# Cross attention on one core: transposing the probabilities by transfers of 16-bit halves instead of on TensorE

## The chip, the core and the metric

The kernel runs on one core of a Trainium2 chip. The metric is the device time of one execution, in microseconds. The core has TensorE (PE, with its weight load shown apart as PEld), VectorE (DVE), ScalarE (ACT), GpSimd (POOL) and SyncE (SP), whose queue issues nearly all transfers of this kernel. Each engine works through its instructions in order; semaphores tie the engines together.

## The reference

The program is one layer of three parts on a latent array x of 16 batches x 64 latents x 512: cross attention to a context of 16 x 512 x 512, a differential self attention over the 64 latents, and a feed-forward with blockwise 4-bit quantisation of activations and weights. Only the first part is touched. With 8 heads of 64, per batch:

```python
xn = _ln(x, g_x, b_x)            # context, 512 rows
ln = _ln(latents, g_l, b_l)      # 64 rows
q = ln @ w_q
kv_in = jnp.concatenate([xn, ln], axis=1)
k, v = jnp.split(kv_in @ w_kv, 2, axis=-1)
sim = jnp.einsum('bhid,bhjd->bhij', q * scale, k)
sim = jnp.where(m, sim, -jnp.finfo(sim.dtype).max)
attn = jax.nn.softmax(sim, axis=-1)
out = jnp.einsum('bhij,bhjd->bhid', attn, v)
return _ln(out @ w_out, g_o, b_o)
```

So each head has 64 queries against 512 context keys and 64 latent keys. The last product contracts over the keys, and TensorE contracts over partitions; the probabilities are computed with the queries on the partitions and must be transposed first. All is float32.

## The kernel before, in words

A first stage (latents) makes the latents' queries, keys and values and parks them in DRAM. Then cross_attention (line 860) loops over the 16 batches, and self attention and feed-forward follow. The order of instructions on each engine is that of the program text; everything below stands where the author of the loop wrote it.

In batch b, PE works through these products. keys(b, m), four times (line 932, tile pk): 12 matmuls of 128x128x512, three terms of a high and low split of float32 over four chunks; DVE evicts the result, times the row of reciprocal deviations (L941). scores(b, a), for a = 0 and 1 (line 957, tile sim): 16 small matmuls each, four heads at a time in two PSUM tiles r = 0, 1, where the partitions are two heads x 64 queries. softmax (line 975): DVE adds the mask and takes the extreme (L986), ACT makes the exponentials and their sum (L990), into the tile pr of 128 x 2 x 576 float32, with the 512 context keys and 64 latent keys of each r in one row. values(b, t), four times (line 944, tile pv): 12 matmuls of 128x128x512, evicted by ACT with a scale (L954).

The products with the values follow one batch later: in batch b, finish(b - 1) (line 1135) does weigh_latents and four times weigh (L1055, tile av), which read the transposed probabilities. These are made in turn(b - 1) (line 994), between keys(b, 0) and keys(b, 1): 32 PE transposes of 64x128 blocks (L1004, tile prt) into the PSUM tiles that the scores use, and four ACT copies (L1013) to the tiles prT in SBUF. turn_latents (line 1016) behind it does the same for the latent keys with two transposes (L1023, tile prlt) and one copy (L1024). In odd batches from 3 on, out_turn (tile ot, copies oh at L1090), and later out_product (tile po) finish a pair of batches.

Beside this run, in the same loop: the next context's split into high and low parts (cx.high on ACT, L362; cx.low on DVE or POOL, L368), the statistics of the context after that on DVE (L321), and the weights' quantiser (Quantise.tick, which advances jobs by one step at each call): a load on SP, then DVE and POOL steps, an ACT step (L205), more DVE, a transposition on DVE (L287), an ACT cast (L288), a subtraction on DVE (L290) and a store on SP (L293).

SP's queue also holds, per batch: four fetches of the raw context (L354), the load of the context in its other layout (nat, L314), the latents' keys (eight small ones, L929 and L930), the row (L347), and in begin(b + 1) the mask bytes mu (L897) and the queries (L899), then the latents' values (L909). ACT turns mu into the mask at the end of the batch (L913).

Pools: pr has two buffers, prT four, the PSUM tiles of pk, pv and po share three, the scores' pair has two.

Of the kernel before, what the change touches and what calls it, by code (L numbers as in the profile page):

```python
# [9 lines left out]
F32 = mybir.dt.float32  # L10
F32R = mybir.dt.float32r
U32 = mybir.dt.uint32
U8 = mybir.dt.uint8
AF = mybir.ActivationFunctionType
ALU = mybir.AluOpType
AX = mybir.AxisListType
# [3 lines left out]
P = 128  # L20
D = 512
KC = D // P
B = 16
S = 64
N = 512
NJ = N // P
# [24 lines left out]
class Common:  # L51
# [808 lines left out]
def cross_attention(tc, cm, sc, i, cw, cx, w1, w2, att, quant):  # L860

    nc = tc.nc
# [24 lines left out]
    state = {}  # L887
    half = (N + S) // 2

    def begin(b):  # L890
        if b >= B:
            return
        p, e = divmod(b, 2)
        g, n = divmod(b, GB)
        mine = slice(n * S, (n + 1) * S)
        mu = w1.tile([P, N], U8, tag="mu", name=f"mu_{b}")
        nc.sync.dma_start(mu, i["mask"][b : b + 1, :].to_broadcast([P, N]))  # L897
        with nc.allow_non_contiguous_dma(reason="the latents of a batch"):
            nc.sync.dma_start(queries[e], sc.q[g][:, :, mine])  # L899
        state[b] = dict(mu=mu, k=[], v=[], tot=cm.small.tile([P, KC], F32, tag="tot", name=f"tot_{b}"))  # L900

    def latents_values(b):
        if b >= B:
            return
        p, e = divmod(b, 2)
        vl = state[b]["vl"] = w2.tile([P, KC, S], F32, tag="two_l", bufs=2, name=f"vl_{b}")
        src = sc.v[p][e * S : (e + 1) * S].rearrange("p (n two d) -> p n two d", two=2, d=S)
        for h in range(2):
            nc.sync.dma_start(vl[h * S : (h + 1) * S], src[:, :, h, :])  # L909
# [22 lines left out]
    def keys(b, m):  # L932

        k = ends.pop((b, m))
        hi, lo = cx.done[b]
        cols = slice(m * P, (m + 1) * P)
        ps = cm.mm(f"pk_{b}_{m}")
        cm.product(
            ps, lambda c: (w_k[0][:, c, cols], w_k[1][:, c, cols], hi[:, c, :], lo[:, c, :]), range(KC)
        )  # L940
        nc.vector.tensor_tensor(k[:, S : S + N], ps, cx.row[b], ALU.mult)  # L941
        state[b]["k"].append(k)

    def values(b, t):
        hi, lo = cx.done[b]
        cols = slice(t * P, (t + 1) * P)
        ps = cm.mm(f"pv_{b}_{t}")
        cm.product(
            ps,
            lambda k: (hi[:, k, cols], lo[:, k, cols], w_v[0][:, k, :], w_v[1][:, k, :]),  # L950
            range(KC),
        )
        v = w1.tile([P, D], F32, tag="v", bufs=4, name=f"v_{b}_{t}")
        nc.scalar.mul(v, ps, cx.rs[b][:, t : t + 1])  # L954
        state[b]["v"].append(v)
# [18 lines left out]

    def softmax(b, a):
        st = state[b]
        st["pr", a] = w1.tile([P, 2, N + S], F32, tag="pr", bufs=2, name=f"pr_{b}_{a}")

        def two(t):
            return t.rearrange("p (h n) -> p h n", h=2)  # L980

        for r, ps in enumerate(st.pop(("sim", a))):
            mask = masks[b % 2][:, columns_of(r)[0]]
            pr = st["pr", a][:, r, :]
            least = cm.small.tile([P, 1], F32, tag="least", name=f"least_{b}_{a}_{r}")
            nc.vector.tensor_tensor_reduce(  # L986
                two(pr), ps[:, :, :half], two(mask), -1.0, BIG, ALU.add, ALU.min, least
            )
            t = 2 * a + r
            nc.scalar.activation(  # L990
                pr, pr, AF.Exp, bias=least, scale=-1.0, accum_out=st["tot"][:, t : t + 1]
            )

    def turn(b):

        pts = [cm.two(f"prt_{b}_{a}") for a in range(2)]
        for a, pt in enumerate(pts):
            for r in range(2):
                first = columns_of(r)[1].start
                for j in range(NJ):  # L1000
                    at = (r * NJ + j) * S
                    for c in range(2):
                        rows = slice(c * S, (c + 1) * S)
                        nc.tensor.transpose(  # L1004
                            pt[:, c, at : at + S],
                            state[b]["pr", a][rows, r, first + j * P : first + (j + 1) * P],
                            cm.ident[rows, rows],
                        )
        for a, pt in enumerate(pts):
            for r in range(2):  # L1010
                prT = w1.tile([P, NJ, P], F32, tag="prT", bufs=4, name=f"prT_{b}_{a}_{r}")
                src = pt[:, :, r * NJ * S : (r + 1) * NJ * S].rearrange("p c (j q) -> p c j q", q=S)
                nc.scalar.copy(prT.rearrange("p j (c q) -> p c j q", q=S), src)  # L1013
                state[b]["prT", a, r] = prT

    def turn_latents(b):
        st = state[b]
        prl = w2.tile([P, 2, P], F32, tag="two_h", bufs=2, name=f"prl_{b}")
        pt = cm.ps_av.tile([P, D], F32, tag="av", name=f"prlt_{b}")[:, : 2 * P]
        pt = pt.rearrange("p (n q) -> p n q", q=P)  # L1020
        for a in range(2):
            pr = st.pop(("pr", a)).rearrange("p r t -> p (r t)")
            nc.tensor.transpose(pt[:, a, :], pr[:, N : N + P], cm.ident)  # L1023
        nc.scalar.copy(prl, pt)  # L1024
        st["prl"] = prl

    def weigh_latents(b):

# [92 lines left out]
    def out_moments(p):  # L1121
        cm.shift(cm.x[p], f"a_{p}", cm.x_mv[:, p, :])
# [29 lines left out]
    for b in range(B):  # L1152

        def tick():
            if b:
                quant.tick()

        done = (b - 3) // 2 if b >= 3 and b % 2 else None
        last = b == B - 1
        keys(b, 0)  # L1160
        if last:
            att.load("Wq")
            att.load("Wk")
        cx.high(b + 1, 0)
        if b >= 4 and b % 2 == 0:
            out_moments((b - 4) // 2)
        if b > 1:
            tick()
        if b:
            turn(b - 1)  # L1170
            turn_latents(b - 1)
        if done is not None:
            out_turn(done)
        keys(b, 1)
        cx.low(b + 1, 0)
        cx.high(b + 1, 1)
        if b > 1:
            tick()
        keys(b, 2)
        if done is not None:  # L1180
            out_low(done)
        cx.fetch(b + 2, 0)
        if b == 0:
            for k in range(KC):
                load_o(k)
        cx.flat(b + 1)
        cx.low(b + 1, 1)
        cx.high(b + 1, 2)
        tick()
        if last:  # L1190
            att.split("Wq", 0, 1)
        if b == 0:
            scores(b, 0)
            softmax(b, 0)
        keys(b, 3)
        cx.fetch(b + 2, 1)
        if b:
            scores(b, 0)
            softmax(b, 0)
        cx.low(b + 1, 2)  # L1200
        cx.high(b + 1, 3)
        if b:
            finish(b - 1)
            scores(b, 1)
            softmax(b, 1)
            around(b + 1, 2, 3)
            around(b + 2, 0, 1)
        tick()
        values(b, 0)
        cx.every(b + 1)  # L1210
        cx.low(b + 1, 3)
        cx.stats(b + 2, 0)
        tick()
        if last:
            att.split("Wq", 2, 3)
            att.load("Wv")
        if b == 0:
            scores(b, 1)
            softmax(b, 1)
            around(b + 1, 2, 3)  # L1220
            around(b + 2, 0, 1)
        values(b, 1)
        begin(b + 1)
        latents_values(b + 1)
        cx.fetch(b + 2, 2)
        cx.stats(b + 2, 1)
        tick()
        if last:
            att.norm(0)
            att.split("Wk", 0, 1)  # L1230
        tick()
        if done is not None:
            out_product(done)
        tick()
        values(b, 2)
        cx.fetch(b + 2, 3)
        cx.stats(b + 2, 2)
        tick()
        if done is not None:
            out_norm(done)  # L1240
            out_add(done)
        if b == 0:
            weight_o(0)
            weight_o(1)
        if b == 2:
            att.sa.load()
        if b == 5:
            att.sa.work()
        if last:
            att.split("Wk", 2, 3)  # L1250
            att.load("Wo")
            att.turn(0)
        values(b, 3)
        cx.stats(b + 2, 3)
        cx.spread(b + 2)
        mask(b + 1)
        if b == 0:
            weight_o(2)
            weight_o(3)
        quant.tick()  # L1260
        cx.load(b + 3)
# [693 lines left out]
```

## Time and profile before

| What | Value |
|---|---|
| Median of 3 runs | 879.98 us (879.5 to 880.17) |
| The profiled execution | 881.33 us |
| Its span, first to last instruction | 879.5 us |
| PE, PEld busy | 871.7 us (99%), 719.2 us (82%) |
| DVE, ACT, POOL busy | 687.2 us (78%), 398.8 us (45%), 296.2 us (34%) |
| PE prt L1004, 512 transposes | 226 ns each, pipelined; 2% of the chain that ended last |
| PE pv and pk L121 | 20% and 19% of that chain |
| ACT copies prT L1013, 64 | 594 ns each |
| SP's queue (q1) | 80136 packets, 109.48 MB, 38.2% of 16 engines |

The engines' times are those of one profiled execution; busy time of PE is that of pipelined matmuls, so what one of many in a row costs is read from the length of the row, not from the mean of one. The chain that ended last is followed back from the last instruction: what stands on it sets the end. The table of groups gives, for a line and an engine, the number, the busy time, the mean of one, and the idle time of the engine just before with what ended it. The first transposes stand at 110 us, the last at 553 us of the span.

### The profile page before, as it was taken

What the parts mean: (1) busy time and instruction counts of PE and PEld (TensorE: products, weight loads), DVE (VectorE), ACT (ScalarE), POOL (GpSimd) and SP (SyncE); (2) the same over time, 40 slices, a digit from 0 to 9 for tenths busy, and PEclk for the clock granted to TensorE, in tenths of its full rate; (3) what the DMA queues carried; (4) which work ended last, traced back from release to release, by engine and by line L of the source; (5) the groups of instructions that cost most, each with busy time, mean ns of one, the idle gap of its engine ahead of it and who ended that gap; (6) DMA issues with size and microseconds to landing.
All of it is one profiled execution on the core that took longest, in us unless ns stands there. A gap on an engine that the chain in (4) does not pass through costs nothing.

```text
span 879.5 us, 17521 instructions
## 1 busy us (share of the span) xinstructions
PE 871.7 (99%) x6743; PEld 719.2 (82%) x6743; DVE 687.2 (78%) x1457; ACT 398.8 (45%) x787; POOL 296.2 (34%) x341
## 2 busy tenths in 40 slices
PE   8999999999999999999999999999999999999998
PEld 8988787878787888778878888888888888888887
DVE  7734457789788887787888867688998897888876
ACT  5654454544544535354445455554556233332221
POOL 2334234235353352353433622545543120111100
PEclk9999999999999999999999999999999999999999
DMA  8464554644655455435644362240008330000000
GB/s 277 167 233 169 167 163 142 201 143 141 192 164 160 138 174 168 136 111 178 183 134 149 121 198 64 82 192 1 1 3 320 136 144 13 13 13 13 13 12 25
DMA packets 80379, 111.12 MB, mean 126 GB/s; under 512 B 33176, under 2 KB 39080, under 8 KB 79016
## 3 DMA queue, kind: packets, MB, share of 16 engines
q1 hardware_dynamic: 80136, 109.48, 38.2%
q8 instruction: 53, 0.87, 0.4%
q0 software_dynamic: 160, 0.52, 0.2%
q14 instruction: 30, 0.25, 0.1%
HBM read 84.26 MB, written 25.72 MB: 125 GB/s over the span
## 4 chain that ended last, share of the span: by engine, by line
PE 93%; DVE 3%; DMA 2%; ACT 1%; POOL 1%; issue 1%; SPq 0%; ACTq 0%; DVEq 0%; POOLq 0%
PE pv L121 20%; PE pk L121 19%; PE gu L121 13%; PE dn L121 6%; PE sim L967 4%; PE av L1055 4%; PE Wv L121 3%; PE wo L121 3%; PE po L121 2%; PE Wq L121 2%; PE Wk L121 2%; PE prt L1004 2%; PE lq L121 2%; PE lk L121 2%; PE lv L121 1%; PE ht L171 1%
## 5 line engine op out<-in xcount | busy, mean ns | idle before, releaser
L121 PE MATMUL pv<-xvh,x 128*128 128x512 f32 x512 | 133.0, 394 | 0.0
L121 PE MATMUL pk<-x,xkh 128*128 128x512 f32 x512 | 128.2, 392 | 0.0
L121 PEld LDWEIGHTS pv<-xvh,x 128*128 128x128 f32 x512 | 94.8, 188 | 26.2 <-issue 7.0
L121 PEld LDWEIGHTS pk<-x,xkh 128*128 128x128 f32 x512 | 94.9, 188 | 19.5 <-issue 0.4
L990 ACT ACTIVATE pr<-pr,least 128x576 f32<-128x576 f32 x64 | 49.1, 769 | 59.7 <-DVE least L986 59.7
L941 DVE TENSOR_TENSOR k<-pk,row 128x512 f32<-128x512 f32 x64 | 43.2, 675 | 39.2 <-PE pk L121 39.0
L368 POOL TENSOR_TENSOR x<-raw,x 128x512 fp32r<-128x512 f32 x32 | 41.6, 1301 | 85.8 <-ACT x L362 80.5
L121 PE MATMUL pv<-xvl,x 128*128 128x512 f32 x256 | 68.7, 390 | 0.0
L121 PE MATMUL pk<-x,xkl 128*128 128x512 f32 x256 | 68.5, 389 | 0.0
L954 ACT ACTIVATE v<-pv,rs 128x512 f32<-128x512 f32 x64 | 43.2, 684 | 54.8 <-PE pv L121 54.3
L121 PE MATMUL gu<-uT,fx 128*128 128x512 f32 (+1 forms) x288 | 67.0, 377 | 0.2 <-DMA uT<-u_d 0.2
L121 PE MATMUL gu<-gT,fx 128*128 128x512 f32 (+1 forms) x288 | 65.8, 376 | 0.0
L121 PEld LDWEIGHTS gu<-gT,fx 128*128 128x128 f32 x288 | 52.2, 188 | 7.6 <-ACT fx L129 0.2
L121 PEld LDWEIGHTS gu<-uT,fx 128*128 128x128 f32 x288 | 51.8, 188 | 7.7 <-DMA uT<-u_d 0.5
L121 PEld LDWEIGHTS pv<-xvl,x 128*128 128x128 f32 x256 | 48.0, 188 | 10.3
L121 PEld LDWEIGHTS pk<-x,xkl 128*128 128x128 f32 x256 | 48.1, 188 | 10.2
L986 DVE CUSTOM_DVE_ANT_0 pr<-sim,mask 128x576 f32<-128x576 f32 x64 | 45.8, 753 | 5.3 <-PE sim L967 4.3
L205 ACT ACTIVATE qe_h<-qe_h,mmagic 128x512 f32<-128x512 f32 (+1 forms) x24 | 16.5, 687 | 66.7 <-DVE qe_h L202 64.6
L321 DVE BATCH_NORM_STATS2 cst<-nat 128x6 f32<-128x512 f32 x64 | 42.8, 669 | 3.7 <-DMA nat<-in_ctx_dram 3.7
L121 PE MATMUL dn<-dT,hh 128*128 128x512 f32 x170 | 42.9, 392 | 0.0
L967 PE MATMUL sim<-k,mask 64*64 64x288 f32 x512 | 40.4, 415 | 0.3 <-DMA mask<-q_d 0.3
L362 ACT CAST x<-raw 128x512 fp32r<-128x512 f32 x64 | 39.1, 631 | 0.0
(347 smaller groups left out, 1867.1 us busy)
## 6 DMA issues: line engine op xcount, KB each, us to landing
nat<-in_ctx_dram SPq DMA_DIRECT2D x16, 1024.0 KB
raw<-in_ctxT_dram SPq DMA_DIRECT2D x64, 256.0 KB
d_d<-qhl_d SPq DMA_DIRECT2D x11, 512.0 KB
row<-rs_d SPq DMA_DIRECT2D x16, 256.0 KB
g_d<-qhl_g SPq DMA_DIRECT2D x8, 512.0 KB
u_d<-qhl_u SPq DMA_DIRECT2D x8, 512.0 KB
gT<-g_d SPq DMA_DIRECT2D x4, 1024.0 KB
uT<-u_d SPq DMA_DIRECT2D x4, 1024.0 KB
```

The costliest lines, as they stand in the source:

```text
L121: self.nc.tensor.matmul(ps, lhsT=p[i], rhs=p[j], start=start and n == 0, stop=stop and n == last)
L205: nc.scalar.activation(e, e, AF.Relu, bias=self.mmagic, scale=MAGIC)
L321: nc.vector.bn_stats(st, self.nat[b][:, j, :])
L362: self.cm.nc.scalar.copy(self.done[b][0][:, c, :], self.raw[:, c, :])
L368: by.tensor_tensor(lo, self.raw[:, c, :], f32(hi), ALU.subtract)
L941: nc.vector.tensor_tensor(k[:, S : S + N], ps, cx.row[b], ALU.mult)
L954: nc.scalar.mul(v, ps, cx.rs[b][:, t : t + 1])
L967: nc.tensor.matmul(pss[r][c * S : (c + 1) * S, h, :half], lhsT=queries[b % 2][rows, m, :], rhs=st["k"][m][rows, at : at + half], start=Tru ...
L986: nc.vector.tensor_tensor_reduce(two(pr), ps[:, :, :half], two(mask), -1.0, BIG, ALU.add, ALU.min, least)
L990: nc.scalar.activation(pr, pr, AF.Exp, bias=least, scale=-1.0, accum_out=st["tot"][:, t : t + 1])
L1004: nc.tensor.transpose(pt[:, c, at : at + S], state[b]["pr", a][rows, r, first + j * P : first + (j + 1) * P], cm.ident[rows, rows],)
L1055: nc.tensor.matmul(st["av"][r][rows, a, :], lhsT=prT[:, j, rows], rhs=st["v"][j][:, at : at + S], start=False, stop=j == NJ - 1, skip_grou ...
```

## The change

For batches 0 to 14, turn is no longer called. Instead, ACT splits the float32 probabilities of pr into two tiles of their low and high 16 bits (halves: two copies of 128 x 1024 words per a). SP issues a transposing transfer for each of the two (send), from 128 x 1024 words to eight transposed blocks of 128 x 128 in a tile far, which takes its place in pr's pool, and so its buffer. In the next batch ACT copies the transposed words back into their places in prT (join: four copies of 128 x 512 words per a), which weigh reads as before. A block's partitions are again the keys, its columns two heads x 64 queries. The last batch still uses turn.

pr and far are now one width (2 x 640 words), so that the context keys of both r can be seen as one regular pattern. turn_latents moves one batch earlier, behind values(b, 1), since pr's buffer is to be freed for far; its result is kept in the second half of the tile that holds the latents' values.

```diff
@@ latents_values(b)
-        vl = state[b]["vl"] = w2.tile([P, KC, S], F32, tag="two_l", bufs=2, name=f"vl_{b}")
+        both = w2.tile([P, 2, KC * S], F32, tag="two_l", bufs=2, name=f"lat_{b}")
+        vl = state[b]["vl"] = both[:, 0].rearrange("p (n d) -> p n d", d=S)
+        state[b]["prl"] = both[:, 1].rearrange("p (n q) -> p n q", q=P)
@@ softmax(b, a)
-        st["pr", a] = w1.tile([P, 2, N + S], F32, tag="pr", bufs=2, name=f"pr_{b}_{a}")
+        wide = w1.tile([P, 2 * (N + 2 * S)], F32, tag="pr", bufs=2, name=f"pr_{b}_{a}")
+        st["wide", a] = wide.rearrange("p (r n) -> p r n", r=2)
+        st["pr", a] = wide[:, : 2 * (N + S)].rearrange("p (r n) -> p r n", r=2)
@@ new functions
+    def halves(b, a):
+
+        st = state[b]
+        src = st.pop(("wide", a))[:, :, :N].bitcast(U16).rearrange("p r (n h) -> p h r n", h=2)
+        for h in range(2):
+            half = w2.tile([P, 2, N], U16, tag="two_h", bufs=2, name=f"half_{b}_{a}_{h}")
+            nc.scalar.copy(half, src[:, h])
+            st["half", a, h] = half
+
+    def send(b, a):
+
+        st = state[b]
+        far = w1.tile([P, 2 * (N + 2 * S)], F32, tag="pr", bufs=2, name=f"far_{b}_{a}")
+        far = far[:, : 2 * N].bitcast(U16).rearrange("p (h n q) -> p h n q", h=2, q=P)
+        for h in range(2):
+            half = st.pop(("half", a, h)).rearrange("p r n -> p (r n)")
+            nc.sync.dma_start(far[:, h], half, transpose=True)
+        st["far", a] = far
+
+    def join(b, a):
+
+        far = state[b].pop(("far", a))
+        for r in range(2):
+            prT = w1.tile([P, NJ, P], F32, tag="prT", bufs=4, name=f"prT_{b}_{a}_{r}")
+            dst = prT.bitcast(U16).rearrange("p j (q h) -> p h j q", h=2)
+            for h in range(2):
+                nc.scalar.copy(dst[:, h], far[:, h, r * NJ : (r + 1) * NJ])
+            state[b]["prT", a, r] = prT
@@ the loop over b, behind keys(b, 0)
         if b:
-            turn(b - 1)
-            turn_latents(b - 1)
+            join(b - 1, 0)
         if done is not None:
             out_turn(done)
         keys(b, 1)
+        if b:
+            join(b - 1, 1)
@@ behind values(b, 0)
+        if b and not last:
+            halves(b, 0)
@@ behind values(b, 1)
+        if b == 0:
+            halves(b, 0)
+        if not last:
+            turn_latents(b)
+            send(b, 0)
         begin(b + 1)
@@ behind values(b, 2)
+        if not last:
+            halves(b, 1)
+            send(b, 1)
```

More of the change, by code (lines that the diff above doesn't have):

```diff
@@ L13 @@
 U8 = mybir.dt.uint8
+U16 = mybir.dt.uint16
 AF = mybir.ActivationFunctionType
@@ L1014, in turn @@
                 state[b]["prT", a, r] = prT
+    def halves(b, a):
[21 more added lines that the diff above has]
+            state[b]["prT", a, r] = prT
     def turn_latents(b):
         st = state[b]
-        prl = w2.tile([P, 2, P], F32, tag="two_h", bufs=2, name=f"prl_{b}")
+        prl = st["prl"]
         pt = cm.ps_av.tile([P, D], F32, tag="av", name=f"prlt_{b}")[:, : 2 * P]
@@ L1024, in turn_latents @@
         nc.scalar.copy(prl, pt)
-        st["prl"] = prl
     def weigh_latents(b):
```

## The prediction

> **What bounds the kernel now.** I read the page first, then the chain of work that ended last in order of time, then the stretch that holds the cross-attention loop.
>
> ```profile
> PE 871.7 (99%) x6743; PEld 719.2 (82%) x6743; DVE 687.2 (78%) x1457; ACT 398.8 (45%) x787; POOL 296.2 (34%) x341
> ```
>
> TensorE (PE) is busy 99% of the span. The chain confirms that this is no average over idle stages: in the loop it never leaves PE. One even batch (6) of it:
>
> ```profile
> 254.91 2.72 PE pk L121 x12
> 257.63 1.14 PE prt L1004 x32
> 259.14 8.21 PE pk L121 x36
> 268.71 2.02 PE av L1055 x64
> 271.86 11.15 PE pv L121 x48
> 283.00 2.72 PE pk L121 x12
> ```
>
> The columns are start, length, what. The batch takes 283.00 - 254.91 = 28.09 us; the odd batch after it, with the output product, 314.57 - 283.00 = 31.57 us; the mean is 29.8. The 32 probability transposes (prt) stand on this chain with 1.14 us; the 0.37 us behind them are the latents' two transposes (prlt), which the change keeps. Before another engine is charged, its room must be known:
>
> ```profile
> 111.00:553.00 442.00, 442.00 (x3732) 355.09 (x3730) 350.37 (x785) 216.76 (x437) 177.01 (x195) 1.00 0.50 154
> ```
>
> This is the stretch of the loop: its length, then busy us (and instructions) of PE, its weight load, DVE, ACT, POOL, the clock, the DMA share, GB/s. PE 442 of 442; ACT 216.76, 49%; DVE 79%; the DMA engines half. The clock is 1.00 throughout, so no clock effect enters.
>
> **Removed.** Fifteen of the sixteen calls of turn (batch 15 keeps its own): 15 x 1.14 = **17.1 us** of PE, all on the path. On ACT, four copies out of PSUM per batch, 2.04 us as a train. The scores' PSUM pair is no longer borrowed; no view shows PE waiting for it, so that is worth nothing.
>
> **Added on ACT.** Nothing in this trace copies 16-bit words with a stride, so I take the rows with the same number of elements:
>
> ```profile
> L1013 ACT COPY prT<-prt 128x512 f32<-128x512 f32 x64 | 32.6, 594 | 0.0
> L362 ACT CAST x<-raw 128x512 fp32r<-128x512 f32 x64 | 39.1, 631 | 0.0
> L1456 ACT ACTIVATE ex<-ex 128x1024 f32<-128x1024 f32 x8 | 8.5, 1062 | 22.6 <-DVE ex L1447 22.6
> ```
>
> Behind one another they overlap: four copies of 594 ns run in 2.04 us, two casts in 1.18 us. halves: 4 x (1.062 - 0.084) = 3.9 us a batch. join: 8 x 0.59 = 4.7 us. Net 3.9 + 4.7 - 2.04 = +6.6 us a batch; ACT goes to 216.8 + 15 x 6.6 = 316 us of some 425, 74%. Bounds: half that time if narrow words run faster, twice if stride or width hurts. Twice would give 216.8 + 15 x (17.2 - 2.0) = 445 us, more than the stretch, and ACT would be the bound. I take the rows as they are, because the mask's activation, which reads one-byte words (715 ns, with bias and scale), costs about what the f32 ones of its size do (684 ns).
>
> Where these copies stand decides more than their sum. Let K be the start of a batch's first pk. In the new order ACT has behind the last pv: v, mask, one x cast, join 0 (2.4), in odd batches four oh (1.2), join 1 (2.4). That ends at K+8. PE needs the last joined tile after four pk (10.9), the first scores (1.1) and the latents' product: K+12.5. Cover: some 4.5 us. In batch 7 of the trace ACT reached its copies only at K+8, since in its order it stood behind a quantiser cast that waited for DVE:
>
> ```profile
> 290.51 0.62 ACT L288 CAST qhl_u<-qhl_u 128x512 fp32r<-128x512 f32 x1 [3.47 <-DVE qhl_u L287]
> 291.04 2.04 ACT L1013 COPY prT<-prt 128x512 f32<-128x512 f32 x4
> ```
>
> So even there join ends near K+13.5, just where weigh takes it. The halves stand behind v of pv 0 and of pv 2, 1.95 us each; the v behind them comes at most 0.3 us later than its pv, and three PSUM buffers cover that. turn_latents now stands behind pv 1 and makes PE wait for the second exp: that ends at about K+19.5, PE arrives at K+21.5. Batch 0 has its second scores only one pv (2.7 us) earlier: up to **+1 us**, once.
>
> **Added transfers.** Four transposes of 128 x 1024 words (256 KB) per batch. The trace holds none. From its packet records, by size: 256-byte packets take 17.9 ns each, 2048-byte ones 101 ns, 4-byte ones 9 ns. A block's row is 128 words, 256 bytes: 1024 packets x 17.9 / 16 engines = **1.15 us**. Low end: like long rows, 128 x 101 / 16 = 0.8 us. High end: each word its own packet, 131072 x 9 / 16 = 74 us. I take 1.15, the packet size that the tile's blocks have. Four make 4.6 us a batch; the DMA share goes from 0.50 to some 0.68.
>
> [...]
>
> On SP's queue, in order, the first pair waits for ACT's halves and for prlt, at K+21.5. It stands where the queue is now, behind the row:
>
> ```profile
> 304.69 0.58 SPq L347 DMA_DIRECT2D row<-rs_d  x1
> 305.31 0.42 SPq L897 DMA_DIRECT2D mu<-in_mask_dram  x1
> ...
> 308.38 0.43 SPq L281 DMA_DIRECT2D qw_g<-in_w_gate_dram  x1
> ```
>
> 304.69 is K+21.7 in batch 7, so hardly a wait; mu, queries, vl, raw and the quantiser's load behind it move back by two issues of 0.6 to 1.2 us. mu is due at the mask, K+28: covered. The second pair waits for the halves behind pv 2 (K+27 to K+30); behind it are a raw fetch (due 14 us later), the quantiser's store and load, and nat. That load took 3.0 us to reach DVE (issue 308.38, use 311.42), and DVE already waited 1 us for it. Landing of a pair: 2 x 1.15 at half-busy engines, 4.6, plus that 3.0 at most: 7.6 us, so the second pair lands near K+7 of the next batch, just ahead of join 1.
>
> **What is late next: DVE.** Its slack in this stretch is what it waits for PE:
>
> ```profile
> DVE k L941 <- PE pk L121: 24.7, 19, 3.6
> ...
> DVE qw_d L207 <- ACT qe_d L205: 3.5, 4, 1.0
> ```
>
> 24.7 for pk and 3.4 for sim are 28 us, 1.9 us a batch; a batch shorter by 1.14 leaves 0.7. Its waits for ACT's part of the quantiser (L207: 3.5 + 3.4 + 3.2; L290: 2.1 + 1.5 + 1.4) are 15 us, 1.0 a batch. ACT's idle share falls from 51% to 26%, so I double them: +1.0 a batch, 0.3 over the slack, some 4.5 us in the loop; the PSUM buffers should swallow part, so I count **+3 us**.
>
> **Sum.** 17.1 - 1 - 3 = 13 us less. The profiled execution took 881.33 us (span 879.5 and 1.8 around it): 868.3. The median of the runs shown is 879.98, 1.35 lower: **867 us**.
>
> **Rivals.**
> Transfers too slow (slower). Place: SP's queue and the 16 engines. Traffic now takes 0.50 x 29.5 = 14.7 us a batch; with four transposes of T it is 14.7 + 4T, and from T = 3.4 us this exceeds the 28.3 us that PE then needs. T = 4.5 gives 32.7 a batch, 3.2 more than now, 15 times: 928 us. For it: the high end of the bound. Against it: the 256-byte row, 1.15.
> DVE and ACT in lockstep (slower). If the quantiser's trips wait 2.6 us more a batch, not 1.0, the batch is 2.6 - 0.7 = 1.9 longer than PE's 28.4 and 0.8 longer than now: 892 us; it turns at 1.8. For it: DVE's slack is small. Against it: the ends of this chain stand mostly in the pv part, where DVE evicts nothing for PE.
> Gain hidden: ACT joins late by just 1.1 us in each batch, PE waits at weigh what it saved: 880 us.
> All of it arrives: 880 - 17 = 863, within my forecast's own range.
>
> **Numbers.** Forecast with its own range 861 to 873: 0.60; a smaller gain, 873 to 878: 0.06; hidden: 0.04; lockstep: 0.14; slow transfers: 0.16. A measurement of this kernel tells 0.2%, 1.8 us, from no change. Faster 0.66, same 0.04, slower 0.30. The range 861 to 900 holds the first three (0.70) and most of the lockstep, about 0.81 in all.
>
> **What would show it.** Right: no prt but batch 15's; pk 0 followed at once by pk 1; batches of 27 and 30.4 us; join and half at 0.5 to 0.6 and 1.0 us; no PE wait for prT; transposes landing within 8 us. Wrong: PE waiting for prT with a transfer behind it (slow transfers); DVE waits for qe or qhl grown beyond 2 us a batch with PE waiting for pk's eviction (lockstep); 16-bit copies at twice the rows.

## The result: 10% slower, and where the profile puts it

The changed kernel takes **968.42 us** (median of 4 runs, 967.33 to 971.93) against 880.08 us for the kernel before on the same chip: a ratio of 1.101, interval 1.098 to 1.104. The forecast was 867, the range 861 to 900. Of the prediction's cases only the one of slow transfers, 928, lay beyond that range, and 968 lies beyond it too. The profiled execution took 969.01 us, its span is 967.2.

The top of the page of the changed kernel: busy time by engine, the granted TensorE clock in 40 slices, and the shares of the chain that ended last.

```profile
PE 895.7 (93%) x6263; PEld 723.4 (75%) x6263; DVE 682.6 (71%) x1457; ACT 497.9 (51%) x907; POOL 295.8 (31%) x341
...
PEclk9999998999899989899989999899999999999999
...
PE 55%; DVE 12%; ACT 11%; DMA 10%; SPq 7%; issue 3%; POOL 1%; DVEq 0%; ACTq 0%; POOLq 0%
```

PE has 480 instructions fewer and is busy 24 us longer: its matmuls were slowed, which the clock row says too (0.963 in the mean of the span, 1.000 before). The chain, which before lay on PE for 93% of the span, now lies there for 55%; for over a quarter of the span it runs through SP's queue, transfers and ACT (7, 10 and 11%). The stretch from the start of the loop to close to its end, in the columns that the prediction used:

```profile
108.00:617.00 509.00, 451.16 (x3180) 348.29 (x3178) 331.72 (x760) 303.86 (x535) 170.03 (x191) 0.94 0.61 161
```

PE idles 509.0 - 451.2 = 58 us here, where it idled none, at a clock of 0.94. The last of batch 15's own transposes, which mark the end of the loop, starts at 553.2 before and at 641.2 now: all of the 88 us is in the loop. What PE, DVE and SP waited for in the loop (us in total, times, longest), from one view for each engine:

```profile
PE pk L122 <- DVE k L944: 17.4, 9, 4.0
PE sim L970 <- DVE least L991: 16.9, 8, 3.7
PE pk L122 <- DVE oz L156: 13.2, 6, 3.5
PE pk L122 <- ACT v L957: 9.8, 5, 3.6
```

```profile
DVE qm_g L195 <- DMA qw_g<-in_w_gate_dram: 20.5, 7, 6.7
DVE qm_d L195 <- DMA qw_d<-in_w_down_dram: 17.6, 6, 5.3
DVE qm_u L195 <- DMA qw_u<-in_w_up_dram: 17.0, 6, 6.4
...
DVE qhl_u L288 <- DMA u_d<-qhl_u: 12.3, 4, 4.7
...
DVE qhl_g L288 <- DMA g_d<-qhl_g: 10.5, 3, 5.7
```

```profile
SPq L355 <- DVE x L369: 51.9, 12, 5.4
SPq L343 <- DVE rsT L340: 42.5, 13, 7.8
SPq L1037 <- PE prlt L1057: 29.4, 11, 4.7
...
SPq L1037 <- ACT mask L916: 17.5, 7, 3.0
...
SPq L1037 <- ACT lat L1058: 12.1, 12, 1.4
```

Read upwards, this is the loss. SP's two longest waits, for the raw context's buffer (L355) and for the deviations that make the row (L343), are no news: before they were 59.7 and 46.8 us. New are those at the transposes (L1037). All rows there add up to 69 us, but some of them count time in which the first transpose of a pair was already being issued. By the gaps in SP's own timeline, SP stands 47 us ahead of the 30 pairs, 32 of it ahead of the first pair of a batch, and the 60 issues themselves hold it for 89 us more. Behind the transposes stand the quantiser's loads and stores. DVE waits 55 us for those loads and 39 for the stores (94 in all; 20.6 before), and PE waits for what DVE does next: the eviction of pk (L944), the scores' minimum (L991), the output's normalisation (L156). Not one PE wait for prT is in this list: the joined tiles are in time. Batch 2, where one such wait for a load reaches PE (timeline, rows of four engines; in brackets the idle time before an instruction and its releaser):

```profile
131.99 0.58 SPq L348 DMA_DIRECT2D row<-rs_d  x1
132.87 2.64 SPq L1037 DMA_TRANSPOSE far<-half  x2
135.55 0.66 SPq L898 DMA_DIRECT2D mu<-in_mask_dram  x1
...
138.86 0.42 SPq L282 DMA_DIRECT2D qw_g<-in_w_gate_dram  x1
139.39 2.95 SPq L1037 DMA_TRANSPOSE far<-half  x2
...
142.44 0.69 DVE L195 TENSOR_REDUCE qm_g<-qw_g 128x32 f32<-128x512 f32 x1 [6.68 <-DMA qw_g<-in_w_gate_dram]
...
145.34 0.62 ACT L289 CAST qhl_g<-qhl_g 128x512 fp32r<-128x512 f32 x1 [6.67 <-DVE qhl_g L288]
145.87 0.68 ACT L957 ACTIVATE v<-pv,rs 128x512 f32<-128x512 f32 x1
146.60 3.78 PE L122 MATMUL pk<-x,xkh 128*128 128x512 f32 x8 [3.62 <-ACT v L957]
```

The same load in batch 2 of the kernel before, on SP and on DVE:

```profile
126.84 0.58 SPq L347 DMA_DIRECT2D row<-rs_d  x1
...
130.51 0.43 SPq L281 DMA_DIRECT2D qw_g<-in_w_gate_dram  x1
...
133.72 0.69 DVE L194 TENSOR_REDUCE qm_g<-qw_g 128x32 f32<-128x512 f32 x1 [0.91 <-DMA qw_g<-in_w_gate_dram]
```

From row to this load SP now needs 138.86 - 131.99 = 6.87 us; before it was 130.51 - 126.84 = 3.67. Of the 3.2 us between, 2.9 are the pair of transposes and the wait ahead of it. The row itself is late by another 3.0 us: it goes out 5.4 us ahead of the batch's first pk (137.39), before 8.4 us (135.24). So the load goes out 6.2 us late against PE, DVE stands 6.68 us in place of 0.91, ACT stands 6.67 us in its own order at a cast that needs DVE, with v behind it, and PE waits 3.62 us for v's PSUM buffer. Then eight matmuls take 3.78 us in place of 1.98: the granted clock is 0.50 from 146 to 152 us.

### The profile page after: what moved, and what is told of

Its sections match the earlier page's. It is cut to its first block, busy times and chain, and to the rows that moved or that the text cites. A ratio compares the mean times of both kernels' runs of the same rounds, so it can differ in the third digit from the quotient of the medians.

```text
span 967.2 us, 16809 instructions
## 1 busy us (share of the span) xinstructions
PE 895.7 (93%) x6263; PEld 723.4 (75%) x6263; DVE 682.6 (71%) x1457; ACT 497.9 (51%) x907; POOL 295.8 (31%) x341
## 4 chain that ended last, share of the span: by engine, by line
PE 55%; DVE 12%; ACT 11%; DMA 10%; SPq 7%; issue 3%; POOL 1%; DVEq 0%; ACTq 0%; POOLq 0%
PE gu L122 13%; PE pk L122 7%; PE dn L122 6%; PE pv L122 4%; ACT prT L1047 3%; PE sim L970 3%; SPq L1037 3%; PE Wv L122 2%; PE wo L122 2%; PE lv L122 2%; ACT half L1027 2%; PE Wq L122 2%; PE Wk L122 2%; DMA u_d<-qhl_u 2%; PE lq L122 2%
## 5 line engine op out<-in xcount | busy, mean ns | idle before, releaser
L122 PE MATMUL pk<-x,xkh 128*128 128x512 f32 x512 | 141.0, 421 | 40.5 <-DVE k L944 17.4
L122 PEld LDWEIGHTS pk<-x,xkh 128*128 128x128 f32 x512 | 101.1, 202 | 71.1 <-DVE k L944 22.6
L122 PE MATMUL pv<-xvh,x 128*128 128x512 f32 x512 | 141.9, 411 | 0.0
L122 PEld LDWEIGHTS pv<-xvh,x 128*128 128x128 f32 x512 | 98.6, 197 | 29.3 <-issue 9.5
L1047 ACT COPY prT<-far 128x512 uint16<-128x512 uint16 x120 | 78.6, 767 | 0.0
L122 PE MATMUL pk<-x,xkl 128*128 128x512 f32 x256 | 73.0, 409 | 0.0
L970 PE MATMUL sim<-k,mask 64*64 64x288 f32 x512 | 50.2, 456 | 21.2 <-DVE least L991 21.2
L1027 ACT COPY half<-pr 128x1024 uint16<-128x1024 uint16 x60 | 59.6, 1040 | 5.8 <-DMA far<-half 5.8
L122 PEld LDWEIGHTS pk<-x,xkl 128*128 128x128 f32 x256 | 51.5, 201 | 11.6
L944 DVE TENSOR_TENSOR k<-pk,row 128x512 f32<-128x512 f32 x64 | 42.5, 665 | 21.6 <-PE pk L122 21.6
L970 PEld LDWEIGHTS sim<-k,mask 64*64 64x64 f32 x512 | 20.4, 142 | 40.7 <-DVE least L991 26.6
L991 DVE CUSTOM_DVE_ANT_0 pr<-sim,mask 128x576 f32<-128x576 f32 x64 | 45.8, 751 | 2.5 <-PE sim L970 1.5
```

The costliest lines, as they stand in the source:

```text
L122: self.nc.tensor.matmul(ps, lhsT=p[i], rhs=p[j], start=start and n == 0, stop=stop and n == last)
L970: nc.tensor.matmul(pss[r][c * S : (c + 1) * S, h, :half], lhsT=queries[b % 2][rows, m, :], rhs=st["k"][m][rows, at : at + half], start=Tru ...
L991: nc.vector.tensor_tensor_reduce(two(pr), ps[:, :, :half], two(mask), -1.0, BIG, ALU.add, ALU.min, least)
L1027: nc.scalar.copy(half, src[:, h])
L1047: nc.scalar.copy(dst[:, h], far[:, h, r * NJ : (r + 1) * NJ])
```

## The experiments

Three theories at the start. **Queue**: transposes at the head of SP's queue, waiting and holding, delay the quantiser's transfers, and DVE with them. **ACT**: halves and joins delay what DVE and PE want of ACT. **Traffic**: the transposes' small packets slow the other transfers. All times are medians; ratios are to the kernel before, measured beside each (879.84 to 881.36 us).

**1. No transfers.** Halves and joins run; the joins copy pr's own words, so the weights are not transposed.

```diff
-            nc.sync.dma_start(far[:, h], half, transpose=True)
...
+        src = st.pop(("wide", a))[:, :, :N].bitcast(U16)
+        st["far", a] = src.rearrange("p r (n q h) -> p h r n q", h=2, q=P)
```

> No transfers: ACT takes the halves apart as in the changed kernel, and join fills prT from pr's own words; the probabilities are not transposed. So ACT's added work is whole and SP's queue is that of before. Theory queue (the transposes stand in SP's order ahead of the quantiser's loads and stores, DVE waits for these, PE for DVE): about 866 to 880 us, no DVE wait for qw or qhl beyond that of before (some 20 us in the loop). Theory ACT (the 120 + 60 copies delay the quantiser's ACT steps and the eviction of pv): over 930. Theory traffic (the transposes' packets slow the other transfers): as theory queue.

Measured: 889.98 us, 1.0114 [1.0085, 1.0143]. So the transfers carry 78 of the 88 us; but neither theory had this size: ACT's copies alone still make the kernel slower than before.

**2. Transfers alone.** A constant tile is transposed straight into prT; halves and joins are left out.

```diff
+            nc.sync.dma_start(far, fixed, transpose=True)
+            state[b]["prT", a, r] = prT
```

> Transfers alone: the same four transposes per batch at the same places of SP's queue, but of a constant tile straight into prT; halves and join are left out, so the probabilities are a constant. SP does not wait for halves or prlt any more, only its 1.3 us per transpose stay. Theory queue: between, 875 to 925, the part of the holding alone; what is missing up to 968 is the waiting at the queue's head, and ACT. Theory ACT: 863 to 868. Theory traffic: 940 or more, as the packets are the same.

Measured: 917.1 us, 1.0422 [1.038, 1.0465]; DVE's waits for the quantiser's transfers are 87 us up to 600. The transfers bring them without any ACT work, and almost without a wait on SP: it stands 2 us ahead of these transposes, and they hold it for 107 us.

**3. The quantiser's transfers on POOL's queue.** The full computation; nothing else changed.

```diff
-        nc.sync.dma_start(w, src)
+        nc.gpsimd.dma_start(w, src)
...
-        nc.sync.dma_start(dst[:, :, k, :], f32(hl))
+        nc.gpsimd.dma_start(dst[:, :, k, :], f32(hl))
```

> The changed kernel whole, with the quantiser's loads and stores issued on POOL's queue instead of SP's. Theory queue: DVE's waits for qw and qhl transfers (94 us in the loop of the changed kernel) fall to a third or less, 875 to 910 us. Theories ACT and traffic: 955 or more.

Measured: 892.56 us, 1.0143 [1.0114, 1.0173]. The transposes are all sent, with the same packets, and 76 us are back. DVE's waits for those transfers fall to 22 us, before's size. That carries the queue theory and speaks against traffic.

**4. Transposes later in SP's queue.** The full computation: the first pair is sent behind the fetch and the quantiser's step that follow pv 2, the second at the end of the batch, behind the load of the context of batch b + 3.

```diff
             turn_latents(b)
-            send(b, 0)
...
             halves(b, 1)
-            send(b, 1)
...
         cx.stats(b + 2, 2)
         tick()
+        if not last:
+            send(b, 0)
...
         cx.load(b + 3)
+        if not last:
+            send(b, 1)
```

> The changed kernel whole, but each pair of transposes is issued later: the first behind the step of the quantiser that follows values(b, 2), the second at the end of the batch, behind the load of the next context. What stood behind them in SP's queue now stands ahead. Theory queue: 880 to 920 us, DVE's waits for the quantiser's transfers halved at least; what stays is that the transposes land later and join may wait. Theories ACT and traffic: 955 or more.

Measured: 924.36 us, 1.0505 [1.0474, 1.0535]. The DVE waits for the quantiser's transfers are back at before's size (21.5 us), which gives back 44 us, yet 44 us of loss remain: ACT now stands 46.2 us at the halves until the late transposes have read the buffers (5.8 in the changed kernel), DVE waits 11.2 us for a cast of ACT's, and PE 5.0 us for prT. DVE's waits for the quantiser's relu and cast are about as long as in the changed kernel or longer (24 and 23 us, there 25 and 19). On one queue a later place helps those in front and makes the transposes late instead; how the 44 us divide was not tested.

**5. Control: the kernel before with POOL's queue for the quantiser** (the edit of experiment 3 on the kernel before).

> A control: the kernel before, with the loads and stores of the quantiser's pieces issued from POOL's queue and nothing else changed (the computation is whole). If the 76 us that this move gave back in the changed kernel came from taking the pieces out from behind the transposes (the queue theory), then here, where no transpose stands in SP's queue, it gives little: 872 to 884 us. If SP's queue was too full already before the change, so that the move is a gain of its own and the changed kernel only hid it, this run goes to 865 us or below. If the issues of 0.6 to 0.7 us each on POOL cost what they take there, it goes above 888.

Measured: 882.02 us, 1.0019 [1.0009, 1.0029]. The move is worth nothing by itself; what it gave in experiment 3 is what the transposes had cost.

**6. No transfers, POOL's queue** (experiments 1 and 3 together).

> The changed kernel without its 60 transfers (the halves are copied, and the joins copy pr's own words, so the weights are not transposed: it leaves out the transposition) and with the quantiser's transfers on POOL's queue. The ACT theory, by which the copies of halves and joins are what is left of the loss, puts it at 885 to 893 us, near the 890.0 without transfers on SP and the 892.6 with them on POOL: neither the transfers nor the queue is in that remainder. If the remainder were still SP's queue (the wait for the latents' transposes at its head), it falls to 863 to 872. DVE's waits for ACT's relu and cast of a piece should be as long as without transfers, some 30 us in the loop.

Measured: 898.35 us, 1.0199 [1.017, 1.0229]. Some 6 us above the kernel that does send its transfers on this queue. The 120 joins take ACT the same time in both (78.8 and 79.1 us), so the reason stays open; the remainder is in the copies, not in transfers.

**7. Transfers alone, POOL's queue** (experiments 2 and 3 together).

> The transposes alone, of a constant tile (halves and joins are left out, so the weights are not the probabilities), with the quantiser's transfers on POOL's queue. The queue theory, by which transposes cost time only through what is queued behind them, puts it at 862 to 872 us, close to the 863 that the removal of the 15 groups of PE transposes should leave of 880. The traffic theory (1024 packets of 256 bytes a transpose on the 16 DMA engines slow the other loads) keeps it at 885 or more, since every packet is still sent.

Measured: 876.81 us, 0.9964 [0.9937, 0.999]. The cost of the transfers is gone to within 4 us of the base found in experiment 13, but it is not 863: something in that figure was wrong as well.

**8. An ordinary copy in place of each transpose**, same place, same waits, same bytes; the weights are not transposed.

```diff
-            half = st.pop(("half", a, h)).rearrange("p r n -> p (r n)")
-            nc.sync.dma_start(far[:, h], half, transpose=True)
+            half = st.pop(("half", a, h)).rearrange("p r (n q) -> p (r n) q", q=P)
+            nc.sync.dma_start(far[:, h], half)
```

> The changed kernel with an ordinary copy of the same bytes, half to far, in place of each transpose, at the same place in SP's queue and behind the same waits (the weights are then not transposed: it leaves out the transposition). If what costs is that SP stands waiting at the head (for the latents' transposes on PE, for the halves), it stays at 940 to 970 us. If it is that a transpose holds the queue for 1.25 to 2.5 us where a plain issue takes about 0.6, it falls to 905 to 930. If it is the transposes' small packets, it falls to the 890 of no transfers at all.

Measured: 945.08 us, 1.0733 [1.0707, 1.0759]. Only 23 us come back. The larger part stays with ordinary copies, which share two things with the transposes: SP stands at the head of its queue for halves and latents (35.4 us for half, 30.0 for prlt in its SP waits), and the 60 issues hold it, though for 36 us instead of 89.

**9. Halves on POOL** (on experiment 3, the full computation).

```diff
-            nc.scalar.copy(half, src[:, h])
+            nc.gpsimd.tensor_copy(half, src[:, h])
```

> The whole computation, the quantiser's transfers on POOL's queue, and the halves copied by POOL in place of ACT. The ACT theory: ACT loses 58 us of copies in the loop, and its waits of 14.6 us for the transposes before them, DVE's waits for ACT's relu and cast fall back towards before's, and the time goes to 872 to 884 us from 892.6. If POOL becomes the bound (its own steps of the quantiser come later, or its copies take more than about 2 us each), it stays at 890 or goes above.

Measured: 929.01 us, 1.055 [1.0526, 1.0575]. A miss: a half takes POOL 1.07 us, about what it takes ACT (1.04), but POOL stands 25.2 us before the copies for the exponentials and 17.7 for the transposes' buffers, and the quantiser's steps and transfers are queued behind it. DVE's waits for the relu are 33 us, against 21 in experiment 3. It looks like the failure of SP's queue, moved; no run separates its parts.

**10. The quantiser's cast on POOL** (on experiment 3, the full computation).

```diff
-        nc.scalar.copy(hi, f32(lo))
+        nc.gpsimd.tensor_copy(hi, f32(lo))
```

> The whole computation, the quantiser's transfers on POOL's queue, and the quantiser's cast of the high word done by POOL, so that one of the two round trips of a piece from DVE to ACT no longer stands behind halves and joins. If DVE's waits for ACT are what is left (the ACT theory in its form DVE and ACT in lockstep), the time falls by a third to a half of the remaining 30 us: 876 to 885. If what is left lies in ACT's own work for PE (v, the exponentials), it stays at 888 to 894.

Measured: 903.98 us, 1.0267 [1.0231, 1.0302]; worse. DVE's waits for the relu fall (12 us from 21), those for the quantiser's transfers rise (28 from 22), and 8.5 us of waiting for POOL's part of the output come up at L146: POOL's order is no freer.

**11. and 12. Joins alone, halves alone** (on experiment 6: no transfers; without joins the weights are a constant tile).

```diff
     def halves(b, a):
+        return
```

```diff
     def join(b, a):
...
-            prT = w1.tile([P, NJ, P], F32, tag="prT", bufs=4, name=f"prT_{b}_{a}_{r}")
...
-                nc.scalar.copy(dst[:, h], far[:, h, r])
-            state[b]["prT", a, r] = prT
+            state[b]["prT", a, r] = still
```

> No transfers and no halves: only the joins (of pr's own words, so the weights are not transposed), quantiser on POOL's queue. ACT gets 8 copies of about 0.65 us a batch in place of 2.04 us of copies from PSUM, net +3.1 us a batch, at the head of the batch. If each microsecond of ACT costs alike, it has 3.1 of f's 7.0 net, so 15 of its 35 us above 863: 878. If the place decides and the joins stand where nobody waits for ACT: 864 to 870. If the joins are the whole loss: 893 or more.

> No transfers and no joins: only the halves run, the weights come from a constant tile, quantiser on POOL's queue. ACT gets 4 copies of 1.04 us a batch and loses 2.04 us, net +1.9 us a batch, in the stretch of the pv products. If each microsecond costs alike: 871 to 874. If the place decides and the halves delay the quantiser's relu and cast and with them DVE: 882 to 895, near f. If they delay nobody: 862 to 866.

Measured: joins alone 897.17 us, 1.0188 [1.0169, 1.0207]; halves alone 877.81, 0.9958 [0.9937, 0.9979]. The joins are the whole of ACT's loss, the halves cost nearly nothing. By their amount of work (3.1 and 1.9 us a batch net) they would have shared it, so either the place counts or the 863 is wrong.

**13. Neither halves, transfers nor joins** (constant weights, POOL's queue).

> No halves, no transfers, no joins: the weights come from a constant tile, PE's 15 groups of transposes and ACT's copies of them are gone and nothing stands in their place; quantiser on POOL's queue. If all of PE's 17 us arrive when nothing else is in the way: 862 to 866 us, and halves alone (877.8) and transfers alone (876.8) each cost some 12. If part of the 17 us was never to be had, because DVE's or POOL's chain is next: 871 to 877, and halves alone and transfers alone cost almost nothing.

Measured: 873.34 us, 0.992 [0.9894, 0.9947]. This is what taking PE's transposes away can give here: 7 us, not 17. Halves alone cost 4 over it, transfers alone 3, joins alone 24; the first two are within the spread of these runs (870.6 to 878.0 here).

**14. and 15. The joins moved, all their work kept** (on experiment 3, the full computation): spread in four pairs; or the first pair's four at the end of their own batch, the second pair's in two pairs around the second tick.

```diff
         if b:
-            join(b - 1, 0)
+            join(b - 1, 0, (0,))
...
         keys(b, 1)
-        if b:
-            join(b - 1, 1)
...
+        if b:
+            join(b - 1, 0, (1,))
         keys(b, 2)
...
+        if b:
+            join(b - 1, 1, (0,))
         tick()
+        if b:
+            join(b - 1, 1, (1,))
```

```diff
-        if b:
-            join(b - 1, 0)
...
         keys(b, 1)
         if b:
-            join(b - 1, 1)
+            join(b - 1, 1, (0,))
...
             tick()
+        if b:
+            join(b - 1, 1, (1,))
         keys(b, 2)
...
         values(b, 3)
+        if not last:
+            join(b, 0)
```

The third argument of join names the r whose tile is filled.

> The whole computation, quantiser on POOL's queue, the eight joins of a batch issued in four pairs, before and after pk 1 and before and after the tick behind pk 2, in place of two fours around pk 1. The same ACT work. If the place decides (a quantiser's relu or cast stands up to 2.4 us behind four joins, DVE with it, and DVE's evictions for PE behind that): 878 to 886 us. If the amount of ACT work decides: 889 to 895, as without spreading.

> The whole computation, quantiser on POOL's queue, the joins of the first pair moved to the end of the batch that made them, behind v 3, and those of the second pair in two pairs before and behind the second tick. If the place decides, since DVE evicts nothing for PE in the pv part: 876 to 884 us. If the amount decides: 889 to 895. If ACT then waits for the first transfer there, it shows as ACT waits at the joins and costs more than 895.

Measured: spread 884.85 us, 1.0048 [1.0027, 1.0069]; early **876.27 us**, 0.9955 [0.9938, 0.9971]. The same copies cost 16 us less at another place, and the kernel is a little faster than before. Early joins also free the buffer of far earlier, but in experiment 3 no DVE wait for that buffer stands in its view, so the place is what is left. Spread helps half: DVE's waits are as short, but the last pair comes late, and PE waits 9.6 us for prT.

**16. Three buffers for the halves** (on the early version), so that the second pair's halves need not wait for the first transposes. Two tiles of later parts of the program, which share these buffers, get three with them.

```diff
-            half = w2.tile([P, 2, N], U16, tag="two_h", bufs=2, name=f"half_{b}_{a}_{h}")
+            half = w2.tile([P, 2, N], U16, tag="two_h", bufs=3, name=f"half_{b}_{a}_{h}")
```

> As the run before (joins early, quantiser on POOL's queue), with three buffers for the halves in place of two, so that the second pair's first half doesn't wait on ACT for the first transposes to have read theirs (14.6 us of ACT waits in the loop without this). If those waits delay DVE as the joins do: 3 to 8 us below the run before. If they lie where nobody needs ACT: within 2 us of it.

Measured: 875.38 us, 0.9939 [0.9921, 0.9957]; not told from the run before. Those waits lie where nobody needs ACT.

**17. and 18. Early joins with the quantiser back on SP's queue**: with the transposes, and with ordinary copies in their place (the weights are then not transposed).

> The whole computation with the early joins of the 876 us version, and the quantiser's transfers back on SP's queue, behind the transposes. If queue and joins are two losses that add: 876 + 76 = 952, so 940 to 960 us. If both act on the same thing, DVE late for PE's evictions, and the queue costs what it costs transfers alone (917 against 877, 40 us): 908 to 925. If the joins at the head of the batch were the whole matter and the queue only met them: 876 to 885.

> The run before with ordinary copies of the same bytes in place of the transposes, at the same place in SP's queue and behind the same waits (the weights are not transposed). What it is faster than the run before is the price of the transposes' hold of the queue (1.25 to 2.5 us each against about 0.6) and of their packets; what it is slower than 876 is the price of SP standing behind waits for ACT's halves and PE's latents. If the waits carry most, as the 945 against 968 with late joins says (23 of 76): within 10 to 25 us of the run before. If the hold carries most: 880 to 890.

Measured: 936.36 us, 1.0618 [1.0594, 1.0642], and 909.82 us, 1.0326 [1.0307, 1.0346]. The queue costs 936 - 876 = 60 us even with the joins well placed. 26.5 of it goes when ordinary copies take the transposes' place, by hold and packets; 33.5 remains, when SP waits and issues ordinary copies. So more stays than goes, as the first case said, though 26.5 is just above its 10 to 25. These are not two parts that add up: in experiment 2, where SP hardly waits ahead of the transposes, hold and packets alone cost 40 us (917 against 877 in experiment 7).

What the runs give together. The last three columns are DVE's waits in the loop (108 to 600, for the changed kernel to 620), in us: for the quantiser's transfers, for its relu (L208) and for its cast (L291), each summed over the rows of the three weights.

| kernel | us | transfers | relu | cast |
|---|---|---|---|---|
| before | 880 | 20.6 | 10.1 | 5.0 |
| changed | 968 | 94.2 | 24.8 | 18.8 |
| transfers alone | 917 | 87.1 | 10.3 | 5.1 |
| quantiser on POOL's queue (3) | 893 | 22.1 | 21.0 | 12.0 |
| the same, joins alone (11) | 897 | 23.8 | 28.3 | 5.8 |
| the same, halves alone (12) | 878 | 18.7 | 8.9 | 12.4 |
| the same, neither (13) | 873 | 15.7 | 12.4 | 5.0 |
| the same, all, joins early (15) | 876 | 19.8 | 10.9 | 11.1 |
| joins early, quantiser on SP (17) | 936 | 90.4 | 13.4 | 9.1 |

The transfers' column goes with the queue, the relu's with the place of the joins, the cast's with the halves; and the time follows the first two more than the third. How the relu's wait reaches PE is seen in experiment 3's timeline:

```profile
235.97 0.42 DVE L203 TENSOR_SCALAR qe_g<-qw_g 128x512 uint32<-128x512 uint32 x1
...
236.85 1.13 ACT L1123 ACTIVATE oh<-ot,bv 128x128 fp32r<-128x128 f32 x4
...
237.85 2.67 ACT L1047 COPY prT<-far 128x512 uint16<-128x512 uint16 x4
...
240.87 0.75 ACT L206 ACTIVATE qe_g<-qe_g,mmagic 128x512 f32<-128x512 f32 x1
...
241.65 1.26 DVE L208 SCALAR_TENSOR_TENSOR qw_g<-qe_g,qw_g 128x512 f32<-128x512 f32 x1 [2.39 <-ACT qe_g L206]
...
243.55 0.68 DVE L944 TENSOR_TENSOR k<-pk,row 128x512 f32<-128x512 f32 x1
...
244.83 0.75 DVE L991 CUSTOM_DVE_ANT_0 pr<-sim,mask 128x576 f32<-128x576 f32 x1
244.96 1.86 PE L970 MATMUL sim<-k,mask 64*64 64x288 f32 x16 [2.02 <-DVE least L991]
```

DVE wrote qe_g by 236.4; ACT takes it at 240.87, behind four joins, four oh and a cast. In its order DVE stands 2.39 us at L208, the eviction of pk 3 is queued behind it, then the first scores' minimum, and PE waits 2.02 us to write the second scores. With the joins early, the longest of PE's waits in the loop are down to these:

```profile
PE sim L970 <- DVE least L991: 1.9, 3, 0.8
PE pk L122 <- ACT v L957: 0.8, 3, 0.3
PE av L1088 <- ACT prT L1047: 0.6, 1, 0.6
```

## Why the prediction was wrong, point by point

**The step that failed is the one on SP's queue.** It listed what stands behind each pair, the quantiser's store and load among it, and knew that DVE already waited 1 us for that load. It priced the mask, the raw fetch and the landing, and gave no price to the load and the store: DVE's extra waits were counted for ACT alone. "Hardly a wait" for the first pair was wrong as well: SP stands 32 us ahead of the 15 first pairs, 2.1 us each and up to 4.8, and 15 ahead of the second ones. The pieces cost 76 us as the kernel stands (968 to 893), 60 with the joins early (936 to 876). Part is the queue held: a transpose kept SP 1.25 to 2.5 us, not "0.6 to 1.2 us" an issue; the other part is standing at waits (89 and 47 us of SP's time in the changed kernel).

```profile
L1037 SPq DMA_TRANSPOSE far<-half x60: 1252/1328/2507, 109.7 to 604.5; - x60
```

These are the changed kernel's transposes on SP's queue, minimum, median and maximum in ns. The ordinary copies of experiment 18 in their place:

```profile
L1037 SPq DMA_DIRECT2D far<-half x60: 493/541/1272, 110.8 to 550.3; - x60
```

**The removal** was right in size and wrong in worth: 17.1 us of PE went, and experiment 13 shows 10.7 less in its profiled execution (870.6 against 881.3), the fastest of its five, and 7 in the median. Two terms make up most of the profile's difference. Batch 0's wait at the latents' transposes was put at +1 us; PE waits 1.8 us there, so that the first pk of batch 1 starts at 109.3 and not 107.1 (110.6 in the changed kernel, where the granted clock behind this wait was 0.50 from 105 to 108 us). The latents' transposes that moved ahead of it are 0.4 of these 2.2 us: +1.8. And PE waits 3.2 us for the scores' minimum: 881.3 - 17.1 + 1.8 + 3.2 = 869.2; the last 1.4 us are not assigned.

**ACT's sum** was nearly right: halves 1.04 us each as worked out; joins 2.67 for a train of four, 0.67 each, not 0.59.

```profile
L1047 ACT COPY prT<-far 128x512 uint16<-128x512 uint16 x120 | 78.6, 767 | 0.0
...
L1027 ACT COPY half<-pr 128x1024 uint16<-128x1024 uint16 x60 | 59.6, 1040 | 5.8 <-DMA far<-half 5.8
```

The cover of the joins was right too: PE waits for none. Its fault is that it looked at one customer of ACT. The quantiser's relu stands behind the joins, and DVE in the pk part behind the relu. **DVE's waits for ACT** did about double, as taken (15 to 33 us in experiment 3), but were priced at 3 us as a mean against a mean slack; at the head of the batch they cost 16 (893 to 876), and 32 with the quantiser on SP's queue (968 to 936). The **lockstep** rival named this mechanism. That its 892 us is what experiment 3 gives is luck: it took 2.6 us more of these waits a batch and a loss only above 1.8, and the runs show (33 - 15) / 15 = 1.2. The reason held against it, that these ends lie mostly in the pv part, is true of the halves, which cost little (878 against 873), and not of the joins, which the change itself put into the pk part.

**The transposes themselves** were close. The loop of experiment 15 has a DMA share of 0.74 over 434 us, that of experiment 13, which sends none, 0.52 over 431: (321 - 224) / 60 = 1.6 us of all 16 engines for each, where 1.15 was estimated. The packets were right, 1024 of 256 bytes for each transpose (61440 more than before in the packet records of the changed kernel); they take some 23 ns each there, not 17.9. The rival of slow transfers (3.4 us and above) falls.

**The clock** was said not to enter. In the kernel before, where PE never waits in the loop, it was 1.00; with the waits it went to 0.94, and pk's matmuls from 392 to 423 ns in the mean. The prediction had no term for this, and it is near half of the loss: PE is busy 895.7 us where 871.7 - 17.1 = 854.6 would be left of before, so the slower matmuls make an estimated 41 us. With the 58 us that PE idles and the 17 saved, that is 82 of the 88.

Settled: the two causes and their places, by undoing each with the other kept (968, 936, 893, 876). Open: how much of the 26.5 us between experiments 17 and 18 is the hold and how much the packets, why experiment 6 is slower than 3, and the last 3 us between experiments 15 and 13.

## What to carry to other kernels

Before a step that waits is put into an in-order queue, list everything queued behind it and who waits for each, and give every one a price, above all those already waited for today: here the quantiser's pieces, off PE's path, carried most of the loss. A slack that is a mean over the loop can't pay for a delay at one place: ask which engine's next instruction stands behind the new work there. The same transfers and copies, with the quantiser on another queue and half of the joins one part earlier, are 0.45% faster than the kernel before (0.9955 [0.9938, 0.9971]).

## What the runs showed of the hardware

In the changed kernel a transpose of 128 x 1024 16-bit words kept SP's queue for 1.25 us at least and 1.33 in the median. With the joins early it was 1.33 in the median again (experiment 17), and an ordinary copy of the same bytes at the same place kept the queue for 0.54 (experiment 18).

Two waits of PE in these runs cost more than their own length. The early version's batch 0, PE alone (four matmuls of pv take 1.07 us in the last row):

```profile
104.34 0.33 PE L1057 MATMUL prlt<-ident,pr 128*128 128x128 f32 x1 [2.59 <-ACT pr L995]
104.42 1.91 PE L122 MATMUL pv<-xvh,x 128*128 128x512 f32 x4
106.13 1.91 PE L122 MATMUL pv<-xvl,x 128*128 128x512 f32 x4
107.83 2.06 PE L122 MATMUL pv<-xvh,x 128*128 128x512 f32 x8
109.73 1.07 PE L122 MATMUL pv<-xvl,x 128*128 128x512 f32 x4
```

Behind 2.59 us of waiting, two groups of four took 1.91 us each, 2 x (1.91 - 1.07) = 1.7 us more than at 1.07; the granted clock from 100 to 110 us was 0.83 in the mean. In the changed kernel a wait of 1.99 us at the same place was followed by slower matmuls too (eight in 3.05 us in place of 1.98, at a granted clock of 0.50 from 105 to 108 us). In experiment 13 none followed a wait of 1.83 us at this place, and the granted clock was 0.999 in the mean of the span:

```profile
103.65 0.33 PE L1044 MATMUL prlt<-ident,pr 128*128 128x128 f32 x1 [1.83 <-ACT pr L995]
103.74 1.17 PE L122 MATMUL pv<-xvh,x 128*128 128x512 f32 x4
104.75 1.08 PE L122 MATMUL pv<-xvl,x 128*128 128x512 f32 x4
```

These are single waits; what decides which of them is followed by slower matmuls was not tested.
